# A decoder layer in fp32 on one core: another order of the second feed-forward matrix's products, a fixed PSUM place for each of their sums, attention output operands made by halves, and the first unit's weight sums shared otherwise between two engines

## The chip, the cores and the metric

One core of a Trainium2 chip runs the whole kernel. The metric is the device time in microseconds of one execution, taken as the median of several runs. The engines that matter are TensorE (PE, with its weight loads PEld), VectorE (DVE), ScalarE (ACT), GpSimd (POOL) and SyncE (SP), which here does nothing but issue DMAs. All data are fp32; a matrix product of fp32 operands shows in the trace as two PE instructions.

## The reference: what is computed

The input `x` has shape (4, 2048, 512): four time steps T, 2048 rows B, 512 features D. One decoder layer is applied:

```python
x = x + ssm(layernorm(x))              # a linear recurrence over the 4 time steps
x = x + cross_attention(layernorm(x), ctx_1024, Wq, Wk, Wv, Wo)   # 16 heads of 32, 77 keys
x = x + ffn(layernorm(x))

def ffn(x):
    h = x @ W_exp + b_exp              # 512 -> 2048
    h = butterfly(h, up_weights)       # 11 stages of 2x2 blocks
    h = gelu(h + up_bias)
    h = butterfly(h, down_weights)
    return h @ W_con + b_con + down_bias   # 2048 -> 512
```

The butterflies are linear, so the kernel first multiplies them into the two matrices. What remains of the feed-forward part is one matrix 512 x 2048, a gelu, and one matrix 2048 x 512.

## The kernel before, in words

**Stages.** A preparation of some 197 us builds the two feed-forward matrices (`_prepare`), keys and values, and the operands of the other projections. Then 16 units follow, each of 128 rows at all four time steps. For unit u, `feed_forward(u, xt, rhs, other)` runs the two feed-forward matrices, and `other` is the generator `front(u + 1, ...)`: recurrence, attention and norm of the next unit. Inside `feed_forward`, `step()` is called after every 4 PE instructions or so, and it advances `other` at a fixed rate, 56 advances over 98 steps (90 in unit 0, which starts with 8 steps without any). So PE alternates between the two units, and each unit takes about 154 us. The last unit, 15, has no `other`.

**Who orders the work.** The program is written in one order, and a scheduler places each engine's instructions from it by their dependencies and by its own idea of durations; each engine then runs its queue strictly in that order. Only in the preparation (PE, SP and POOL) and in the first four columns of unit 0 (PE) is the written order kept, and where `tc.keep_in_program_order` says so.

**First matrix** (`up_head`, `up_mid`, `up_tail`, lines 777 to 826). Eight columns p, seven block products each (Strassen's scheme), with weights of 896 KB from `up7` that SP loads in `up_weights` (L1013). Three accumulators with PSUM tags a, b, c are reused within a column, so PE waits for DVE's reads (L799, L811, L812, L820, L823). ACT applies the gelu (L785).

**Second matrix** (the loop over `plan` in `feed_forward`). 26 products, each 4 fp32 matmuls (8 PE instructions, L876) of 128 x 256. `DOWN` gives their order: the product's number, the name of the sum in PSUM that it is added to, and where that sum then goes ("+20" is row block t = 2, left half of the features, added; two or three targets make one wide DVE instruction). A sum keeps its name over several products, and what comes later under the same name is added on top of what was there: DVE adds the running value to `xt` (L891) or subtracts it (L893), and the next product of that name has to wait until DVE has read. The sum's PSUM place was taken in rotation over the tags a, b, c (two buffers each) when a name first appeared.

The left operands are sums of the activations (`SUMS`, `LEFT`), made on POOL (`made`, L833), 1.3 us each, 28 per unit. `_down_plan` places them: each sum is emitted so that it stands four products ahead of the product that needs it, and it is written to the place that came free first, be it one of nine spare places or the block of an activation that is no longer needed.

The right operands are 26 blocks of the second matrix in DRAM (`dn26`), loaded two by two on SP (L869). They are made only once: `_right_sums` forms 18 sums of blocks for one of four row sets, `_right_stores` writes them to DRAM (L152). Set 0 is done in the preparation, all on POOL (L140); sets 1 to 3 in unit 0 after columns 0 to 2, where the names in `FAST` go to DVE (L142). Both use the same two rings in SBUF, so a set has to wait for the stores of the one before. SP issues these stores ahead of the weights of column 4, since columns 0 to 3 were loaded ahead.

**Attention output** (end of the loop over t in `front`, then `sw`). For each time step ACT computes exponentials (L680), DVE the sums (L678, L682, L683), PE transposes the probabilities (L695) and multiplies by the values into `ps_o` (L705). DVE copies that to `ot` (L707). After the fourth copy, four sums of quarters of `ot` are made, two on DVE (L714, L715) and two on POOL (L716, L717), and the seven products with `wo` follow (L615), whose results DVE adds to `xt` (L724, L728).

**Norm.** `norm_stats` (L536 to L549) is a chain on DVE: four statistics of 128 x 512, then thirteen tiny instructions of 128 x 4 with three Newton steps. `normed` then scales rows (L562), PE transposes them (L571), ACT copies them out (L572). `normed_pairs` does the same for the recurrence (L589, L600, L601). After its own front, each unit from 1 on computes the statistics of the next `x` in advance (`stats`); unit 1's are computed at the start of its front, in unit 0.

**Bias and stores.** The output bias `ybias` is added to `xt` on POOL: quarter rows in each column (L848), in unit 0 two additions of 128 x 1024 in columns 5 and 7 (L851). The result rows are stored from SP (L859): rows 0, 1, 2 after product 17, halves of row 3 after product 6 and at the end. Units' `xt` live in three buffers, so the load of unit u + 2 (L528) waits for the stores of unit u - 1.

Of the kernel before, what the change touches and what calls it, by code (L numbers as in the profile page):

```python
# [14 lines left out]
ALU = mybir.AluOpType  # L15
AX = mybir.AxisListType

P = 128
T, B, D = 4, 2048, 512
# [48 lines left out]
DOWN = ((11, "x", "+01"), (12, "y", "+30"), (5, "x", "+00"), (16, "y", "+31"), (1, "p", "+11"), (18, "q", "+20"),  # L68
# [4 lines left out]

# [7 lines left out]
PLAIN = tuple(f"b{k}{n}" for k in range(4) for n in range(2))  # L81
FAST = "24", "5", "1", "8"
SLOT = {name: i for i, name in enumerate([row[0] for lot in RIGHT for row in lot] + list(PLAIN))}
# [418 lines left out]
def kernel(ctx: ExitStack, tc: tile.TileContext, x, ctx_t, ssm_vec, ssm_vt, ssm_vinv, wq_t, wk_t, wv_t,  # L502
                        wo_t, wexp_t, up_low, up_high, up_bias, dn_low, dn_high, wcon, b_con, down_bias, out):
    nc = tc.nc
# [13 lines left out]
    ybias = const.tile([P, D], F32, name="ybias")  # L518
# [101 lines left out]
    def front(u, xt, res, wq=None):  # L620
# [47 lines left out]
        ot = work.tile([P, NC, T, P], F32, tag="xnt", bufs=2, name="ot")  # L668
        for t in range(T + 1):
# [32 lines left out]
            for g in range(NC):  # L702
                for j in range(4):
                    h = 4 * g + j
                    nc.tensor.matmul(po[j * DH : (j + 1) * DH, g, :], lhsT=vsb[:, tt, h * DH : (h + 1) * DH],  # L705
                                     rhs=pts[0:NK, g, j, :], start=True, stop=True, tile_position=(0, j * DH))
            nc.vector.tensor_copy(ot[:, :, tt, :], po)  # L707
            yield
# [4 lines left out]
        s1, s2, s3, s4 = (sw[:, i] for i in range(4))  # L713
        nc.vector.tensor_tensor(s1, a21, a22, ALU.add)  # L714
        nc.vector.tensor_tensor(s2, s1, a11, ALU.subtract)  # L715
        nc.gpsimd.tensor_tensor(s3, a11, a21, ALU.subtract)  # L716
        nc.gpsimd.tensor_tensor(s4, a12, s2, ALU.subtract)  # L717
        yield
# [32 lines left out]
    def feed_forward(u, xt, rhs, other):  # L751
# [17 lines left out]
        def bank(tag):  # L769
            return psum.tile([P, 512], F32, tag=tag, name=f"ps_{tag}")  # L770
# [64 lines left out]
        for p in range(h):  # L835
# [5 lines left out]
            if u == 0 and p < 3:  # L841
                _right_sums(nc, p + 1, wdn, rings, False)
                _right_stores(nc, p + 1, wdn, rings, dn26, (0, 1, 2))
# [3 lines left out]
            if u:  # L847
                tc.keep_in_program_order(nc.gpsimd.tensor_tensor(r, r, ybias[:, d], ALU.add))  # L848
            elif p % 2 and p > h // 2:
                r = xt[:, p - 5 : p - 3, :]  # L850
                tc.keep_in_program_order(nc.gpsimd.tensor_tensor(r, r, ybias.unsqueeze(1).to_broadcast([P, 2, D]), ALU.add))  # L851
            if p >= h // 2:
                made(*plan.pop(0)[1:])
        up_tail(h - 1)

        sums, banked, pair = {}, 0, None

        def store(t, d=slice(0, D)):
            nc.sync.dma_start(out=out[t, u * P : (u + 1) * P, d], in_=xt[:, t, d])  # L859

        for kind, where, *rest in plan:
# [9 lines left out]
            if first:  # L871
                sums[name] = bank("abc"[banked % 3])[:, 0 : D // 2]
                banked += 1
            ps, left = sums[name], place(where)
# [6 lines left out]
            while goes:  # L881
# [10 lines left out]
                else:  # L892
                    nc.vector.tensor_tensor(r, r, x, ALU.subtract)  # L893
            for t, when in enumerate((17, 17, 17)):
                if i == when:
                    store(t)
            if i == 6:
                store(3, slice(0, D // 2))
        store(3, slice(D // 2, D))
        for _ in other:  # L900
# [28 lines left out]
    with ExitStack() as stack, tc.manual_schedule(engines={E.PE, E.SP, E.Pool}):  # L929
# [45 lines left out]
        for n, _ in enumerate(prep):  # L975
            if n == 27:
                _right_sums(nc, 0, wdn, rings, True)
            if n == 31:
                _right_stores(nc, 0, wdn, rings, dn26, (2, 0))
# [114 lines left out]
```

## Time and profile before

| | us |
|---|---|
| median of 3 runs | 2631.2 (2629.01 to 2632.6) |
| the profiled execution | 2631.95 |
| its span, first to last instruction | 2630.2 |
| mean granted clock of PE | 0.993 |

| stage | from, to (us) |
|---|---|
| preparation, with the front of unit 0 | 0 to 197 |
| unit 0, with the front of unit 1 | 197 to 382 |
| units 1 to 14, some 154 us each | 382 to 2534 |
| unit 15 alone | 2534 to the end |

A line of the profile that groups instructions gives source line, engine, operation, and the program's names of output and inputs (buffer numbers left out). In a view by order of time the first two numbers are the start and the duration in us, and in brackets stands how long the engine was idle before and what ended the idle time. In a view of waits the three numbers are the total in us, how many times, and the longest. In a view by windows each engine's busy time in the window is followed by its number of instructions, and the last three numbers are the granted clock of PE, the mean share in which the DMA engines were busy, and GB/s. Of an engine's idle time only PE's is a loss by itself.

### The profile page before, as it was taken

The numbers are of one execution on the slowest core, as the hardware profiler recorded it, in microseconds if no ns is written. First come the engines' busy times: TensorE is split into PE (matmuls) and PEld (weight loads), VectorE is DVE, ScalarE is ACT, GpSimd is POOL, SyncE is SP. The second block draws the span as 40 slices with busy tenths as digits, with TensorE's granted clock in tenths as the row PEclk, the third lists the DMA queues.
The fourth block names the chain that finished last, engine by engine and source line by source line (L and its number), as shares of the span: only waits on it lengthen the run. The fifth ranks groups of instructions, "written<-read, shape, count | busy, mean of one in ns | idle before, by whom it ended". The sixth has DMA issues, their size and how long they took to land.

```text
span 2630.2 us, 39485 instructions
## 1 busy us (share of the span) xinstructions
PE 2526.9 (96%) x14280; PEld 2126.0 (81%) x14280; DVE 1599.6 (61%) x3480; ACT 1039.9 (40%) x3263; POOL 935.2 (36%) x851
## 2 busy tenths in 40 slices
PE   8896999999999999999999999999999999999999
PEld 5775878787888878788887878888787887878788
DVE  6657475755747575574747557474755747565553
ACT  2442524336262433626244362624436262443621
POOL 4437231514233151423415242341524234152434
PEclk9997999999999999999999999999999999999999
DMA  5718443454535345453544545453454544444456
GB/s 178 254 68 309 143 159 142 156 177 153 200 140 173 144 154 179 153 200 141 166 149 151 184 152 198 143 168 145 151 186 153 196 145 159 149 153 171 154 171 238
DMA packets 143220, 440.71 MB, mean 168 GB/s; under 512 B 20657, under 2 KB 48433, under 8 KB 140209
## 3 DMA queue, kind: packets, MB, share of 16 engines
q1 hardware_dynamic: 143026, 438.18, 48.2%
q8 instruction: 115, 1.88, 0.3%
q14 instruction: 79, 0.65, 0.1%
HBM read 398.27 MB, written 39.86 MB: 167 GB/s over the span
## 4 chain that ended last, share of the span: by engine, by line
PE 76%; DVE 14%; ACT 7%; issue 1%; DMA 1%; POOL 1%; SPq 0%; DVEq 0%; ACTq 0%; POOLq 0%
PE ps_b L780 11%; PE ps_a L876 9%; PE ps_a L780 7%; PE ps_q L615 7%; PE ps_c L780 7%; PE ps_c L876 6%; PE ps_w L615 5%; PE ps_b L876 4%; PE ps_pt L695 3%; PE ps_sc L675 3%; ACT pr L680 3%; PE ps_s L630 3%; PE ps_o L705 3%; PE ps_t L571 2%; DVE st L536 2%; ACT L785 1%
## 5 line engine op out<-in xcount | busy, mean ns | idle before, releaser
L833 POOL TENSOR_TENSOR arena<-arena 128x512 f32<-128x512 f32 x448 | 601.2, 1348 | 1288.8 <-ACT arena L785 780.8
L785 ACT ACTIVATE arena<-arena,hbias 128x256 f32<-128x256 f32 x384 | 191.7, 507 | 338.8 <-DVE arena L820 263.6
L680 ACT ACTIVATE pr<-ps_sc,low 128x77 f32<-128x77 f32 x960 | 297.1, 331 | 48.3 <-DVE low L678 46.0
L780 PE MATMUL ps_b<-arena 128*128 128x256 f32 x1128 | 293.2, 380 | 8.7 <-issue 5.4
L572 ACT COPY xnt<-ps_t 128x512 f32<-128x512 f32 x128 | 72.1, 585 | 474.2 <-PE ps_t L571 474.2
L780 PEld LDWEIGHTS ps_b<-arena 128*128 128x128 f32 x1128 | 207.6, 190 | 40.8 <-issue 10.6
L876 PE MATMUL ps_a<-arena 128*128 128x256 f32 x896 | 223.2, 379 | 0.0
L680 ACT ACTIVATION_READ_ACCUMULATOR pr<-ps_sc,low 128x1 f32 x960 | 203.2, 212 | 0.0
L780 PE MATMUL ps_a<-xnt,arena 128*128 128x256 f32 x752 | 196.4, 380 | 1.3 <-ACT arena L785 1.3
L876 PEld LDWEIGHTS ps_a<-arena 128*128 128x128 f32 x896 | 165.7, 190 | 26.4
L876 PE MATMUL ps_c<-arena 128*128 128x256 f32 x768 | 184.4, 380 | 0.2
L678 DVE TENSOR_REDUCE low<-ps_sc 128x4 f32<-128x308 f32 x240 | 114.8, 478 | 101.5 <-PE ps_sc L675 96.0
L675 PE MATMUL ps_sc<-kbd,qt 128*128 128x308 f32 x480 | 166.6, 434 | 0.0
L876 PE MATMUL ps_a<-w,arena 128*128 128x256 f32 x512 | 133.8, 385 | 30.1 <-DVE xt L893 15.7
L876 PEld LDWEIGHTS ps_c<-arena 128*128 128x128 f32 x768 | 144.0, 190 | 22.8 <-DMA arena<-dn 2.5
L780 PEld LDWEIGHTS ps_a<-xnt,arena 128*128 128x128 f32 x752 | 143.3, 191 | 23.6 <-ACT arena L785 1.6
L796 ACT COPY arena<-ps_a 128x256 f32<-128x256 f32 x128 | 48.2, 376 | 274.6 <-PE ps_a L780 274.6
L615 PE MATMUL ps_q<-xnt,wq 128*128 128x256 f32 x640 | 151.2, 379 | 2.2 <-POOL xnt L660 2.2
L695 PE MATMUL ps_pt<-ident,pr 128*77 128x128 f32 x1024 | 148.6, 278 | 4.0 <-DVE pt L700 4.0
L695 PEld LDWEIGHTS ps_pt<-ident,pr 128*77 128x77 f32 x1024 | 116.9, 147 | 37.6 <-DVE pt L700 10.0
L820 DVE TENSOR_TENSOR arena<-ps_b,arena 128x256 f32<-128x256 f32 x128 | 54.0, 422 | 137.1 <-PE ps_b L780 137.1
L615 PEld LDWEIGHTS ps_q<-xnt,wq 128*128 128x128 f32 x640 | 121.4, 190 | 19.1 <-POOL xnt L660 2.6
(232 smaller groups left out, 5007.2 us busy)
## 6 DMA issues: line engine op xcount, KB each, us to landing
arena<-dn SPq DMA_DIRECT2D x256, 512.0 KB, 4.3
w<-dn SPq DMA_DIRECT2D x160, 512.0 KB, 3.7
arena<-up SPq DMA_DIRECT2D x79, 896.0 KB, 4.5
wq<-wq SPq DMA_DIRECT2D x16, 1792.0 KB, 8.4
w<-up SPq DMA_DIRECT2D x32, 896.0 KB, 6.3
xt<-in_x SPq DMA_DIRECT2D x11, 1024.0 KB, 7.2
dn<-arena SPq DMA_DIRECT2D x8, 1152.0 KB, 5.1
out<-xt SPq DMA_DIRECT2D x33, 256.0 KB, 5.9
```

The costliest lines, as they stand in the source:

```text
L572: nc.scalar.copy(xnt[:, :, t, :], ps)
L615: nc.tensor.matmul(tiles[key][:, r, :], lhsT=lhs(i, r, k), rhs=rhs(i, r, k), start=key == i and r == 0 and k == 0, stop=k == 1, skip_group ...
L630: nc.tensor.matmul(ps[:, 2 * i : T, f * NS : (f + 1) * NS], lhsT=xpt[:, i, c * (P // NS) + f, :], rhs=gt[:, 0 : T - 2 * i, :], start=i == ...
L675: nc.tensor.matmul(ps[:, 0 : 4 * NK], lhsT=qt[:, g, t, :], rhs=kbd[:, t, g, :], start=True, stop=True)
L678: nc.vector.tensor_reduce(low, sc, AX.X, ALU.min)
L680: nc.scalar.activation(pr[:, 4 * g + h, :], sc[:, h, :], AF.Exp, bias=low[:, h : h + 1], scale=-1.0, accum_out=sm[:, 4 * g + h : 4 * g + h ...
L695: nc.tensor.transpose(pt_ps[0:NK, j, :], pr[:, 4 * g + j, :], ident)
L705: nc.tensor.matmul(po[j * DH : (j + 1) * DH, g, :], lhsT=vsb[:, tt, h * DH : (h + 1) * DH], rhs=pts[0:NK, g, j, :], start=True, stop=True, ...
L780: nc.tensor.matmul(ps, lhsT=w[:, c, :], rhs=rhs[i - 1][:, c], start=first and c == 0, stop=c == 1, skip_group_check=True)
L785: nc.scalar.activation(out, x, AF.Gelu, bias=hbias[:, b : b + 1])
L833: nc.gpsimd.tensor_tensor(place(p), place(x), place(y), ALU.add if op == "+" else ALU.subtract)
L876: nc.tensor.matmul(ps, lhsT=left[:, j, :], rhs=pair[:, n, j, :], start=first and j == 0, stop=j == NB // 4 - 1, skip_group_check=True)
```

## The change

1. `DOWN` has another order from the 11th product on, the sum "p2" is called "o", and each sum's PSUM tag is fixed by `BANK` in place of the rotation. The planner's sums follow the new order.
2. In unit 0 the right sums of set 1 go to POOL alone, and `FAST` sends eight names instead of four to DVE in sets 2 and 3.
3. The copy of `ps_o` to `ot` goes from DVE to ACT, and the four sums `s1` to `s4` are made in two halves, for t = 0 and 2 and for t = 1 and 3.
4. In unit 0 the bias additions are eight of 128 x 256, in columns 6 and 7.
5. The statistics of `x` of unit 1 are computed in the preparation.
6. The stores: rows 1 and 2 after product 19, the left halves of rows 0 and 3 after product 6, the right half of row 0 after product 23, that of row 3 at the end.

```diff
-        (22, "r", "+31"), (13, "p2", "+00"), (25, "w", "+00"), (14, "x", "+10 +11"), (3, "v", "+20"),
-        (15, "y", "+21 +20"), (7, "w", "+20"), (24, "v", "+00 +10"), (20, "z", "+31"), (8, "u", "-00 -10"),
-        (9, "w", "+21"), (10, "z", "+11"), (4, "u", "+21"), (21, "s", "+01 +11 +21"), (19, "z", "+10"), (23, "w", "+01"),
-        (17, "t", "+10 +30 -01 -21"), (2, "z", ""), (6, "z", "+30"), (0, "u", "+31"))
+        (22, "r", "+31"), (13, "o", "+00"), (25, "w", "+00"), (14, "x", "+10 +11"), (15, "y", "+21 +20"), (3, "v", "+20"),
+        (20, "z", "+31"), (7, "w", "+20"), (8, "u", "-00 -10"), (10, "z", "+11"), (24, "v", "+00 +10"),
+        (21, "s", "+01 +11 +21"), (17, "t", "+10 +30 -01 -21"), (9, "w", "+21"), (4, "u", "+21"), (19, "z", "+10"),
+        (2, "z", ""), (6, "z", "+30"), (23, "w", "+01"), (0, "u", "+31"))
+BANK = dict(x="a", y="b", p="c", q="c", r="c", o="c", w="a", v="b", z="a", u="b", s="c", t="c")
...
-FAST = "24", "5", "1", "8"
+FAST = "24", "5", "1", "8", "14", "2", "20", "10"
...
-            nc.vector.tensor_copy(ot[:, :, tt, :], po)
+            nc.scalar.copy(ot[:, :, tt, :], po)
...
-        nc.vector.tensor_tensor(s1, a21, a22, ALU.add)
-        nc.vector.tensor_tensor(s2, s1, a11, ALU.subtract)
-        nc.gpsimd.tensor_tensor(s3, a11, a21, ALU.subtract)
-        nc.gpsimd.tensor_tensor(s4, a12, s2, ALU.subtract)
+        for q in (slice(0, 1), slice(1, 2)):
+            nc.vector.tensor_tensor(s1[:, :, q], a21[:, :, q], a22[:, :, q], ALU.add)
+            nc.vector.tensor_tensor(s2[:, :, q], s1[:, :, q], a11[:, :, q], ALU.subtract)
+            nc.gpsimd.tensor_tensor(s3[:, :, q], a11[:, :, q], a21[:, :, q], ALU.subtract)
+            nc.gpsimd.tensor_tensor(s4[:, :, q], a12[:, :, q], s2[:, :, q], ALU.subtract)
...
-                _right_sums(nc, p + 1, wdn, rings, False)
+                _right_sums(nc, p + 1, wdn, rings, p == 0)
...
-            elif p % 2 and p > h // 2:
-                r = xt[:, p - 5 : p - 3, :]
-                tc.keep_in_program_order(nc.gpsimd.tensor_tensor(r, r, ybias.unsqueeze(1).to_broadcast([P, 2, D]), ALU.add))
+            elif p >= h - 2:
+                for t in (2 * p - 12, 2 * p - 11):
+                    for d in (slice(0, D // 2), slice(D // 2, D)):
+                        added = nc.gpsimd.tensor_tensor(xt[:, t, d], xt[:, t, d], ybias[:, d], ALU.add)
+                        tc.keep_in_program_order(added)
...
-                sums[name] = bank("abc"[banked % 3])[:, 0 : D // 2]
-                banked += 1
+                sums[name] = bank(BANK[name])[:, 0 : D // 2]
...
-            for t, when in enumerate((17, 17, 17)):
-                if i == when:
-                    store(t)
+            if i == 19:
+                store(1)
+                store(2)
             if i == 6:
+                store(0, slice(0, D // 2))
                 store(3, slice(0, D // 2))
+            if i == 23:
+                store(0, slice(D // 2, D))
         store(3, slice(D // 2, D))
...
+            if n == 36:
+                stats[1] = norm_stats(xts[1], tc.keep_in_program_order)
```

More of the change, by code (lines that the diff above doesn't have):

```diff
@@ L854, in feed_forward @@
         up_tail(h - 1)
-        sums, banked, pair = {}, 0, None
+        sums, pair = {}, None
         def store(t, d=slice(0, D)):
```

## The prediction

> **What bounds the kernel now.** I read the page's engine shares first, then the waits of the matmul engine by stretch, then one steady unit in order of time on each engine, then the start of the first unit.
>
> ```profile
> PE 2526.9 (96%) x14280; PEld 2126.0 (81%) x14280; DVE 1599.6 (61%) x3480; ACT 1039.9 (40%) x3263; POOL 935.2 (36%) x851
> ```
>
> PE is the bound. No edit changes its instruction count, so all that can be won is its idle time, some 103 us of 2630.2, and the places where its clock is low. Waits of PE from 500 us on, where units 1 to 14 pass the place in question, and unit 15 without another unit beside it:
>
> ```profile
> PE ps_a L876 <- DVE xt L893: 15.7, 9, 1.8
> PE ps_a L876 <- DVE arena L893: 8.7, 5, 1.8
> PE ps_w L615 <- DVE sw L715: 6.8, 13, 0.5
> PE ps_a L876 <- ACT arena L785: 5.4, 13, 0.4
> PE ps_b L780 <- issue: 5.0, 13, 0.4
> PE ps_t L571 <- DVE xn L562: 2.9, 14, 0.2
> PE ps_o L705 <- DVE pt L700: 2.6, 14, 0.2
> ```
>
> Columns: total us, times, longest. Fourteen times PE waits 1.75 us for one VectorE subtraction at L893. Around it, in the unit near 1200 us, PE, then DVE, then POOL:
>
> ```profile
> 1288.10 1.13 PE L876 MATMUL ps_a<-w,arena 128*128 128x256 f32 x4 [1.75 <-DVE xt L893]
> 1289.44 0.63 PE L571 MATMUL ps_t<-ident,xn 128*128 128x128 f32 x4 [0.21 <-DVE xn L562]
> ```
> ```profile
> 1283.64 1.11 DVE L547 TENSOR_TENSOR w<-y,v 128x4 f32<-128x4 f32 x1
> 1284.79 0.16 DVE L548 TENSOR_TENSOR w<-w,y 128x4 f32<-128x4 f32 x1
> 1284.98 1.12 DVE L549 SCALAR_TENSOR_TENSOR y<-w,y 128x4 f32<-128x4 f32 x1
> 1286.14 0.16 DVE L547 TENSOR_TENSOR w<-y,v 128x4 f32<-128x4 f32 x1
> 1286.34 1.11 DVE L548 TENSOR_TENSOR w<-w,y 128x4 f32<-128x4 f32 x1
> 1287.37 0.68 DVE L893 TENSOR_TENSOR xt<-xt,ps_a 128x512 f32<-128x512 f32 x1
> ```
> ```profile
> 1279.53 7.90 POOL L833 TENSOR_TENSOR arena<-arena 128x512 f32<-128x512 f32 x6 [10.78 <-PE ps_b L876]
> ```
>
> PE must add product 4 to the sum "u" that product 8 left; the subtraction that reads it stands on DVE behind the Newton steps of the norm. Of those, every second one takes 1.1 us instead of 0.16, as long as POOL runs its six operand sums. The same chain ends in the row L562 that the transposes need. So two waits lie on each other: take only the first away and PE stands at L571. Last, the start of the first unit, as windows (PE, PEld, DVE, ACT, POOL, clock, DMA share):
>
> ```profile
> 215.00:220.00 5.00, 0.23 (x2) 0.00 (x0) 3.83 (x12) 0.00 (x0) 3.03 (x4) 0.58 0.92 310
> 220.00:225.00 5.00, 1.00 (x5) 1.03 (x6) 4.89 (x9) 0.00 (x0) 4.92 (x7) 0.50 1.04 342
> 250.00:255.00 5.00, 0.06 (x1) 0.09 (x2) 4.86 (x6) 0.00 (x0) 4.12 (x3) 0.50 1.05 443
> ```
>
> Here PE idles for 8.77 us (for xp L589) and 7.15 us (for xn L562), both behind the norm on DVE beside a busy POOL.
>
> **What the Trainium skill says.** "SBUF — State Buffer", Who interferes with whom: a DVE instruction with two SBUF inputs, or in a two-port mode, and a GpSimd instruction that reads SBUF take one port in turn, for a whole instruction. The trace agrees: 0.16 against 1.11 us above, while evictions with one PSUM input keep 0.42. "TensorE: Matmul & The Clock Gate", What's actually happening: an idle window of some 3.4 us halves the clock, and about as much work restores it. Agrees: 0.50 after both stalls, four matmuls in 1.91 instead of 1.03. "VectorE: DVE Perf Modes", The TRN2 errata: copying 512 fp32 from PSUM is (120+512)/0.96 = 658 ns on DVE and (172+512)/1.2 = 570 ns on ScalarE; the trace has 0.69 (L707) and 0.58 (L572).
>
> **The change part by part.**
>
> Product order and fixed places. Each product is 8 PE instructions, 1.73 us; PE reaches L571 in the middle of the 19th product in either order. Before, 8 and 4 stood 16th and 19th with two products between them; now 15th and 21st with five, 8.6 us instead of 3.5. The wait for L893 was 3.5 + 1.75 after product 8 ended, so it goes: 24.4 us. What is late next is the row at L571, ready at 1289.30, where PE without the stall would be at 1287.05: 2.25 us would remain, more than the stall. It depends on POOL. By the planner's rule the new order asks for the sums of the late products (7, 8, 9, 24, 21, 17) from operands and places that come free by the 12th product, so some 16 sums of 1.3 us run from about 1250 to 1266, and POOL then waits for the 18th product (1286.2). Without POOL the thirteen steps L542 to L549 take 0.2 us each, 2.6, as they do at 1303 to 1306, against 6.5 here (7.15 less 0.6 for L893). Five evictions now fall into the chain (0.42, 0.68, 0.42, 0.66, perhaps 0.96) where there were three (0.66, 0.39, 0.68): +0.5 to +1.4. Row at 1289.30 - 3.9 + 1.0 = 1286.4, before PE at 1287.05. So the 2.9 us go too. If half of the sums stay in the window, the row comes at 1287.3 to 1288.4, 0.3 to 1.3 us per unit left.
>
> New wait: 2 follows 19 directly on "z", so its first matmul waits until DVE has evicted 19: 0.42 + about 0.1 if DVE is free, 1.8 more if it stands behind L745 (1.79). Queued behind it on PE: the rest of the unit. PE's order is the scheduler's, which already hoists (the 2nd product runs before the 1st), and 23 or the next unit's first product can go between: 0 to 2.3 us, I take 0.4, 14 x 0.4 = 5.6 back. The other places: "r" needs "p" evicted one product earlier; bounded by one DVE multiply L683 (up to 2.37), hidden by the hoisting; 0.
>
> Operands by step, copy of ot to ScalarE. L615 waits 0.52 for L715 (1.64 us beside POOL L716). Now the halves for t = 0 and 2 are made before the last copy; after it remain 0.58 (ACT), and two halves of 0.41 (as L142), from 1264.3 to 1265.7, or 1267.1 if each meets a POOL half of 0.72 (as L848). PE would want the first half at 1267.03 and this one four matmuls (0.86) later: the wait goes, 7.8 us in all (15). Halves cost 0.13 more each on DVE, 0.17 on POOL, beside PE. The copy takes 0.69 x 64 = 44 us from DVE, puts 37 on ACT; ACT stands idle after each ps_o (0.99, 2.87, 3.07 us and 26 after the last), so 0. Without that cover it would be up to 0.58 x 4 x 15 = 35 us.
>
> Stores: six instead of five on SP per unit; behind them weights that land far ahead: 0, at the end too, since the last store is the same half row (0.3 either way).
>
> First unit. Statistics of x1 move ahead of the first product, into DVE's idle 4.03 us before 197.46 and the 3.28 that L142 leaves there; they cost 5.3 us alone, up to 10 beside POOL; in the second case L799 of the first product is 2 us late. Set 1 of the right sums goes wholly to POOL: 4 more of 0.74; it frees L368, for which PE waits 2.50. Sets 2 and 3 give four more each to DVE (0.41): POOL has 38 instead of 42, 3.0 us less, DVE 16 instead of 12. The bias additions (two of 2.34) become eight of 0.72 and come one step later: +1.1 us of POOL, but shorter blocks of the port. Waits that could go: 2.50 + 8.77 + 7.15, with some 6 us of half clock. But p = 4 needs weights that SP issues behind the nine right-sum stores, at 241.04, landing 4.5 later, 245.6, at most 3.0 earlier; DMA is near full share from 205 to 250. p = 4 starts now at 258.52, so the gain is at most 12.9 to 15.9, less some 2 of half clock after the idle that is left: I take 11, bounds 0 (DVE blocked by L142 waiting for a store) and 16. In the first unit's second matrix the row wait of 2.89 (POOL: four sums, 5.18) goes by 2.6.
>
> **Sum.** 24.4 + 2.9 + 7.8 - 5.6 + 2.6 + 11 = 43.1. From the profiled execution's 2631.95 that gives 2588.9; it lies 0.75 over the median of 2631.2, so 2588.
>
> **The rivals.** One: the row takes the place. POOL's sums stay beside the norm chain, L571 inherits the stall, and only L615 (7.8), 0.3 a unit (4) and half of the first unit (7) are won, 18.8: 2612. For it: both waits end on one DVE chain. Against: the planner's rule. Two: all goes, z is filled, and the small waits of 0.39 on L780 behind L589 go too (5): 29.5 + 5.6 + 5 + 2.6 + 16 = 58.7: 2572. Three, slower: the eviction of 19 stands on DVE behind the next unit's statistics, 7 us long (1298.94 to 1306), and PE waits for it at 2. It decides from 43.1/14 + 0.4 = 3.5 us a unit; at 5 us it is 14 x 4.6 - 43 = 21 slower: 2652. For it: just such a place cost "u" 4.5 us after its product. Against: 19 ends at about 1294, before those statistics. Four: DVE's relief was hidden and the first unit's weights decide; within 5 us.
>
> **Chances.** Forecast 0.56, one 0.21, two 0.13, three 0.06, four 0.04. A measurement here tells 0.2%, 5 us, from none: faster 0.90, same 0.04, slower 0.06. The range of 2567 to 2615 takes in one and two and leaves out three and four.
>
> **What would show it.** Right: no PE wait on L893; L571 waits under 0.3 a unit; L615 none on sw; POOL's sums in one block before L716, none beside L542 to L549; L600's wait of 8.77 and the half clock after it gone, with a wait for weights or rows near 240 to 245. Wrong: L571 with 1 to 2 us a unit, a wait of PE on L891 at the last products, or p = 4 at 255 or later.

## The result, and the profile after

| | before | after |
|---|---|---|
| median | 2632.21 us (20 runs) | 2639.48 us (20 runs, 2635.63 to 2646.15) |
| ratio to before | | 1.0024, interval 1.0013 to 1.0034 |
| the profiled execution, its span | 2631.95, 2630.2 us | 2642.55, 2640.8 us |

Slower by 0.24%, where 1.6% faster was forecast. 2639.5 is outside the range, and of the rivals only the third lies on that side. The shares of the engines, first:

```profile
PE 2537.6 (96%) x14280; PEld 2127.7 (81%) x14280; DVE 1519.4 (58%) x3452; ACT 1071.6 (41%) x3327; POOL 924.2 (35%) x885
```

DVE has lost 80 us and PE has gained 11: that DVE has less to do did not by itself make the kernel shorter. Next the waits of PE from 500 us on, in the same columns (total, times, longest); most lines are one higher than before, those of the feed-forward two or three.

```profile
PE ps_o L706 <- DVE pt L701: 18.1, 26, 1.0
PE ps_a L879 <- DVE xt L894: 11.4, 9, 1.3
PE ps_a L879 <- DVE arena L894: 6.2, 5, 1.3
PE ps_w L616 <- DVE sw L717: 5.0, 13, 0.4
PE ps_c L879 <- DMA arena<-dn: 2.9, 3, 1.7
```

The 24.4 us on the subtraction (L893 before, L896 now) and the 2.9 on L571 are gone, as forecast. In their place stand 17.6 us (11.4 and 6.2) at product 2, which follows product 19 on the sum z, and 18.1 at `ps_o`, which was 2.6. The same unit as before, near 1200 us, on DVE:

```profile
1282.53 0.16 DVE L548 TENSOR_TENSOR w<-y,v 128x4 f32<-128x4 f32 x1
1282.72 0.16 DVE L549 TENSOR_TENSOR w<-w,y 128x4 f32<-128x4 f32 x1
1282.80 0.42 DVE L894 TENSOR_TENSOR xt<-ps_a,xt 128x256 f32<-128x256 f32 x1
1283.14 0.15 DVE L550 SCALAR_TENSOR_TENSOR y<-w,y 128x4 f32<-128x4 f32 x1
...
1293.65 1.79 DVE L747 TENSOR_TENSOR arena<-xnt 128x512 f32<-128x512 f32 x1 [0.70 <-ACT xnt L573]
1295.55 0.69 DVE L749 TENSOR_TENSOR arena<-xnt,arena 128x512 f32<-128x512 f32 x1
1296.15 0.69 DVE L537 BATCH_NORM_STATS2 st<-arena 128x6 f32<-128x512 f32 x1
1296.76 0.41 DVE L894 TENSOR_TENSOR xt<-ps_a,xt 128x256 f32<-128x256 f32 x1
```

Above the dots, the Newton steps: 0.16 us each where every second one took 1.1. That part is right. Below, the last line is the eviction of product 19. It stands behind the combination sums of the next unit's operands (L747, L749) and one of the next unit's statistics, and PE waits for it, after six of the eight instructions of product 23 (the first line):

```profile
1294.50 1.46 PE L879 MATMUL ps_a<-w,arena 128*128 128x256 f32 x6
1297.22 3.07 PE L879 MATMUL ps_a<-arena 128*128 128x256 f32 x13 [1.26 <-DVE xt L894]
```

The sums of POOL, which no longer lie beside the norm, lie here:

```profile
1249.83 9.49 POOL L835 TENSOR_TENSOR arena<-arena 128x512 f32<-128x512 f32 x6 [1.50 <-PE ps_a L879]
1259.29 0.90 POOL L718 TENSOR_TENSOR sw<-ot 128x256 f32<-128x256 f32 x1
1260.16 4.02 POOL L835 TENSOR_TENSOR arena<-arena 128x512 f32<-128x512 f32 x3
1264.14 0.90 POOL L719 TENSOR_TENSOR sw<-ot,sw 128x256 f32<-128x256 f32 x1
```

That is the attention output of the next unit. What lay there in the kernel before, on POOL and then on DVE (the multiply of the softmax, the second operand sum):

```profile
1250.25 9.08 POOL L833 TENSOR_TENSOR arena<-arena 128x512 f32<-128x512 f32 x6 [1.46 <-PE ps_a L876]
1256.26 1.95 DVE L683 TENSOR_TENSOR pr<-pr,sm 128x1232 f32<-128x1232 f32 x1
1265.76 1.64 DVE L715 TENSOR_TENSOR sw<-sw,ot 128x512 f32<-128x512 f32 x1
```

And in after, on DVE, the same multiply and the second halves of the two sums:

```profile
1253.39 1.71 DVE L684 TENSOR_TENSOR pr<-pr,sm 128x1232 f32<-128x1232 f32 x1
1262.03 1.02 DVE L716 TENSOR_TENSOR sw<-ot 128x256 f32<-128x256 f32 x1 [1.49 <-ACT ot L708]
1263.08 1.37 DVE L717 TENSOR_TENSOR sw<-sw,ot 128x256 f32<-128x256 f32 x1
```

So six of POOL's sums lay there before as well; the move made the stretch longer and denser. The two second halves end 2.4 us after the last copy of `ot`, as late as the two whole sums did before. Last, the stretches of the first unit's start in after's windows (columns as before), with the one from 250:

```profile
215.00:220.00 5.00, 4.09 (x24) 3.31 (x23) 4.90 (x8) 0.59 (x1) 4.45 (x6) 1.00 0.93 317
220.00:225.00 5.00, 4.37 (x25) 3.78 (x26) 4.96 (x9) 2.60 (x6) 3.62 (x5) 1.00 0.75 251
250.00:255.00 5.00, 5.00 (x17) 4.06 (x17) 2.56 (x3) 0.94 (x2) 4.35 (x5) 0.69 0.97 388
```

PE works where it stood idle, and the recurrence of unit 1 starts at 221.15 instead of 232.80 us.

**Where the time came from.** A way of counting used below: from PE's records, the time from one instruction's start to the next beyond what is usual for that line and width, summed over a unit and put down to the later one's line. It includes half clock and the filling of the pipeline, so it is more than the waits. A unit's period is the distance from one recurrence to the next; "steady" is its median over units 1 to 13.

| | before | after |
|---|---|---|
| start of unit 0's first product | 197.01 | 193.60 |
| start of unit 1's recurrence | 232.80 | 221.15 |
| period of unit 0 | 160.74 | 162.69 |
| steady period | 153.60 | 154.72 |
| lost at `ps_o`, L706 | 3.11 | 4.39 |
| lost at `ps_w`, L616 | 1.05 | 1.43 |
| lost at scores and transposes, L676 and L696 | 1.49 | 2.43 |
| lost at second matrix, L879 | 2.70 | 2.45 |
| lost at first matrix and norm, L782 and L572 | 1.26 | 0.22 |

So a start 11.7 us earlier is more than spent by 1.1 us in each of the later units, by 2 in unit 0, by 2 in what follows the last recurrence, and by another 1.5 to 2.2 in each of three units where weights landed late.

### The profile page after: what moved, and what is told of

It reads as the page before. It is cut to its first block, busy times and chain, and to the rows that moved or that the text cites. A ratio compares the mean times of both kernels' runs of the same rounds, so it can differ in the third digit from the quotient of the medians.

```text
span 2640.8 us, 39542 instructions
## 1 busy us (share of the span) xinstructions
PE 2537.6 (96%) x14280; PEld 2127.7 (81%) x14280; DVE 1519.4 (58%) x3452; ACT 1071.6 (41%) x3327; POOL 924.2 (35%) x885
## 4 chain that ended last, share of the span: by engine, by line
PE 77%; DVE 10%; ACT 8%; DMA 2%; POOL 1%; issue 1%; DVEq 0%; POOLq 0%; ACTq 0%; SPq 0%
PE ps_a L879 11%; PE ps_b L782 11%; PE ps_a L782 7%; PE ps_q L616 7%; PE ps_c L782 7%; PE ps_b L879 6%; PE ps_c L879 6%; PE ps_w L616 6%; ACT pr L681 4%; PE ps_sc L676 3%; PE ps_s L631 3%; PE ps_pt L696 3%; PE ps_o L706 2%; PE ps_t L572 2%; ACT L787 1%; ACT L681 1%
## 5 line engine op out<-in xcount | busy, mean ns | idle before, releaser
L835 POOL TENSOR_TENSOR arena<-arena 128x512 f32<-128x512 f32 x448 | 593.6, 1336 | 1457.8 <-ACT arena L787 822.3
L782 PE MATMUL ps_b<-arena 128*128 128x256 f32 x1128 | 293.8, 381 | 3.8 <-DVE arena L813 3.8
L879 PE MATMUL ps_a<-arena 128*128 128x256 f32 x896 | 220.0, 381 | 18.8 <-DVE xt L894 12.7
L782 PEld LDWEIGHTS ps_b<-arena 128*128 128x128 f32 x1128 | 209.8, 191 | 31.3 <-DVE arena L813 4.2
L879 PEld LDWEIGHTS ps_a<-arena 128*128 128x128 f32 x896 | 165.5, 190 | 50.0 <-DVE xt L894 16.7
L879 PE MATMUL ps_b<-arena 128*128 128x256 f32 x768 | 201.4, 380 | 0.5 <-DVE xt L894 0.5
L782 PE MATMUL ps_a<-xnt,arena 128*128 128x256 f32 x752 | 196.3, 380 | 0.0
L676 PE MATMUL ps_sc<-kbd,qt 128*128 128x308 f32 x480 | 170.2, 442 | 0.0
L879 PE MATMUL ps_a<-w,arena 128*128 128x256 f32 x640 | 160.9, 382 | 5.9 <-ACT arena L787 5.8
L782 PEld LDWEIGHTS ps_a<-xnt,arena 128*128 128x128 f32 x752 | 143.3, 191 | 22.0
L696 PE MATMUL ps_pt<-ident,pr 128*77 128x128 f32 x1024 | 153.4, 279 | 4.2 <-DVE pt L701 3.9
L616 PE MATMUL ps_q<-xnt,wq 128*128 128x256 f32 x640 | 151.2, 379 | 2.2 <-POOL xnt L661 2.2
L696 PEld LDWEIGHTS ps_pt<-ident,pr 128*77 128x77 f32 x1024 | 119.2, 147 | 41.8 <-DVE pt L701 15.7
L879 PEld LDWEIGHTS ps_b<-arena 128*128 128x128 f32 x768 | 137.6, 190 | 16.0 <-DVE xt L894 0.9
L879 PEld LDWEIGHTS ps_a<-w,arena 128*128 128x128 f32 x640 | 118.8, 190 | 26.8 <-ACT arena L787 11.4
L616 PEld LDWEIGHTS ps_q<-xnt,wq 128*128 128x128 f32 x640 | 121.5, 190 | 19.0 <-POOL xnt L661 2.6
```

The source lines that it names most:

```text
L616: nc.tensor.matmul(tiles[key][:, r, :], lhsT=lhs(i, r, k), rhs=rhs(i, r, k), start=key == i and r == 0 and k == 0, stop=k == 1, skip_group ...
L676: nc.tensor.matmul(ps[:, 0 : 4 * NK], lhsT=qt[:, g, t, :], rhs=kbd[:, t, g, :], start=True, stop=True)
L696: nc.tensor.transpose(pt_ps[0:NK, j, :], pr[:, 4 * g + j, :], ident)
L782: nc.tensor.matmul(ps, lhsT=w[:, c, :], rhs=rhs[i - 1][:, c], start=first and c == 0, stop=c == 1, skip_group_check=True)
L835: nc.gpsimd.tensor_tensor(place(p), place(x), place(y), ALU.add if op == "+" else ALU.subtract)
L879: nc.tensor.matmul(ps, lhsT=left[:, j, :], rhs=pair[:, n, j, :], start=first and j == 0, stop=j == NB // 4 - 1, skip_group_check=True)
```

## The experiments

The theory after the traces, P, is that each unit has three new costs, each with its own cause: (1) the fixed place for "r" takes away a filler ahead of the first `ps_o`; (2) product 2 follows product 19 on its place; (3) POOL's moved sums meet DVE's work of the attention output, halves included. The rival, A, is that the copy of `ot` on ScalarE makes the loss. A third reading is that the first unit's edits win nothing that lasts. The first four kernels undo one part of the change or do one part alone.

**e1: rotation in place of the fixed places.**

```diff
-                sums[name] = bank(BANK[name])[:, 0 : D // 2]
+                sums[name] = bank("abc"[banked % 3])[:, 0 : D // 2]
+                banked += 1
```

> The changed kernel with the rotation over the tags a, b, c put back in place of the fixed places; all else as changed. Theory P (places): with "r" bound to tag c, product 22 can no longer stand ahead of the first attention output product, so PE has nothing to run while DVE copies the transposed probabilities; with the rotation three quarters of product 22 stand there again (1.3 us), the wait of 1.0 us a unit at that place goes, and the time falls by 15 x 1.0 to 1.3, to 2620 to 2625. Rival A (ScalarE copy): the wait comes from the copy of ot that went to ScalarE, and stays: 2637 to 2642.

2626.55 us, ratio to before 0.9975 (0.9966 to 0.9984). Steady 153.89, 0.83 less than after. What filled PE ahead of the first `ps_o` in the kernel before, and what is left of it in after:

```profile
1233.28 0.60 PE L876 MATMUL ps_b<-arena 128*128 128x256 f32 x2
1233.71 1.46 PE L876 MATMUL ps_b<-w,arena 128*128 128x256 f32 x6
1235.10 1.08 PE L705 MATMUL ps_o<-pt,vsb 77*32 77x128 f32 x32
```
```profile
1228.84 0.60 PE L879 MATMUL ps_b<-arena 128*128 128x256 f32 x2
1230.45 1.08 PE L706 MATMUL ps_o<-pt,vsb 77*32 77x128 f32 x32 [1.01 <-DVE pt L701]
```

The six instructions of 1.4 us are three quarters of product 22, "r". With "r" on tag c, behind "p" and "q" on the same tag, its place isn't free yet. With rotation they stand there again and the first `ps_o` has no wait. But the third and the last one now wait, 0.32 and 0.81:

```profile
PE ps_o L706 <- DVE pt L701: 15.9, 28, 0.8
```

So cause (1) is shown, at 0.83 us a unit net. The edit frees the places of all the sums; that it is "r" that counts is read from these lines. Little of the gain is at `ps_o` itself (4.39 to 4.28 lost), since the later ones take up most of what the first one gives; `ps_w` falls from 1.43 to 0.89. The waits at `ps_o` have a second cause.

**e2: the copy of `ot` back on VectorE.** `nc.scalar.copy(ot[...], po)` is `nc.vector.tensor_copy` again.

> The changed kernel with the copy of ps_o to ot back on VectorE; all else as changed. Rival A: the waits at the attention output, at the transposes of the probabilities and at the scores go back to what they were, 2.2 us a unit less: 2606 to 2612. Theory P: the wait of 1.0 us at the first attention output product of a unit stays; only the small losses at the scores and transposes (0.5 and 0.4 us a unit) can go: 2626 to 2636, and the waits of the operand sums for the attention output grow by 0.1 each.

2638.59 us, 1.0027 (1.0017 to 1.0037): as after. Scores and transposes fell back from 2.43 to 1.52 us a unit, and `ps_w` rose from 1.43 to 2.11. `ps_o` rose by 0.21. The copy on ScalarE isn't free: it costs 0.9 where the exponentials and the copies of pt stand on the same queue, and wins about as much at `ps_w` and `ps_o`. Rival A falls. The steady period is 154.57, so the copy explains 0.15 of the 1.1.

**e3: the first unit's edits alone**, in the kernel before: `FAST`, set 1, bias additions, statistics in the preparation.

> The kernel before with the first unit's edits alone: right sums shared otherwise, statistics of unit 1 in the preparation, bias additions in quarter rows; order, places, copy and stores as before. If these edits gave the 11.6 us that the first unit's recurrence comes earlier in the changed kernel, and no unit pays for it later: 2618 to 2623. If the gain is given back in the same unit's second matrix (the next 160.8 us became 162.7): 2621 to 2625. If it came from the order of the products: 2629 to 2634.

2626.85 us, 0.9981 (0.9970 to 0.9992): 6 us are won, though unit 1's recurrence starts at 220.30, 12.5 earlier than in before's trace. Unit 0 is 3.2 longer, the steady period is 153.71.

**e4: order, places and stores alone**, in the kernel before.

> The kernel before with the new product order, the fixed places and the stores that go with it; first unit, copy and operand sums as before. Theory P: the norm's wait at L571 and the wait of 1.75 us for the subtraction go (2.2 us less a unit), 1.0 comes at the first attention output product and some 1.3 at the product that follows product 19 on sum z: within 5 us of 2632. Rival A: no new wait at the attention output: 2610 to 2620. If the step sums and not the order made POOL's sums fall into the attention output, they wait here as before (0.5).

2637.2 us, 1.0019 (1.0011 to 1.0027). Without halves, copies and first unit, the order with its places is by itself slower. Its waits, from 375 us on:

```profile
PE ps_w L616 <- DVE sw L716: 20.8, 14, 1.5
PE ps_o L706 <- DVE pt L701: 14.2, 14, 1.0
PE ps_a L876 <- DVE xt L891: 11.4, 9, 1.3
PE ps_a L876 <- DVE arena L891: 6.2, 5, 1.3
```

All three new costs are here; the third shows as the old wait for the whole sums at `ps_w`, which has grown from 0.52 to 1.49: the first sum (L715 here, L714 before) took 1.67 us beside POOL's sums instead of 0.69. The steady period is 154.29, so in the fixed places the copies and the halves together cost only the 0.43 that remain to after's 154.72. Yet unit 1's recurrence starts at 225.98 in this kernel, which has none of the first unit's edits. More on that at e8.

**e5: 19 four products ahead of 2**, on top of e1 (rows 1 and 2 are stored after 4):

```diff
-        (21, ...), (17, ...), (9, ...), (4, ...), (19, "z", "+10"), (2, "z", ""), (6, "z", "+30"),
+        (21, ...), (19, "z", "+10"), (17, ...), (9, ...), (4, ...), (2, "z", ""), (6, "z", "+30"),
```

> The kernel after with its places dealt out in rotation, and product 19 moved from directly ahead of 2 to a place four products earlier (21, 19, 17, 9, 4, 2); rows 1 and 2 are stored after product 4. Theory P (2 follows 19 on its place, 1.26 us a unit behind the next unit's combination sums on VectorE): the wait at the z products goes, 14 x 1.26 = 17.6, nothing takes its place; a steady period of 152.6 us instead of 153.87, and 2609 us, 17 less than the rotation alone (2626.6). Rival R (VectorE's backlog at that point is what holds PE, so another eviction of the last products or the first of the next unit's expansion inherits the wait): the period stays above 153.4 and the time above 2620.

2609.41 us, 0.9912 (0.9899 to 0.9926), 17 less than e1, as expected. Steady 152.91; the second matrix loses 0.69 instead of 2.52. What remains at that place is 0.3 a unit at the next unit's first product:

```profile
PE ps_a L782 <- DVE xt L895: 2.8, 9, 0.3
PE ps_a L782 <- DVE arena L895: 1.2, 4, 0.3
```

Cause (2) is shown, about 1.0 us a unit net.

**e6: whole sums** on top of e1, s1 to s4 as in the kernel before.

> The kernel after with its places in rotation and the four operand sums of the attention projection made whole, as in the kernel before. Theory Q (the first halves stand on VectorE ahead of the last copy of pt, so the last ps_o waits 0.81 us a unit for them): that wait goes, and ps_w waits for the whole sums instead, 1.0 to 1.5 us a unit; the time within 5 us of the rotation alone (2626.6). Rival S (the last ps_o waits because the softmax multiply on VectorE is drawn out to 2.5 us by GpSimd's sums, whatever the halves do): the wait stays at 0.7 or more and ps_w adds 0.5 to 1.0 to it; 2634 to 2642.

2624.46 us, 0.9965 (0.9952 to 0.9977). `ps_o` loses 3.48 instead of 4.28, `ps_w` 1.36 instead of 0.89: what the halves win at `ps_w` they cost ahead of the last `ps_o`.

**e7: GpSimd kept quiet** on top of e1. From unit 1 on, the kernel leaves out some 18 of the 28 operand sums of a unit, so what it writes is not the layer's result; PE's work is the same.

```diff
             if kind == "sum":
-                made(where, *rest)
+                if not u or done < 3 or done > 17:
+                    made(where, *rest)
```

> The kernel after with its places in rotation, which in units 1 to 15 leaves out the operand sums on GpSimd that the plan puts from the third to the seventeenth product of the second matrix, some 18 of 1.3 us a unit (their operands are what an earlier unit left there). Theory T (these sums, moved out of the norm's chain, now draw out VectorE's work in the attention output): the multiply L684 falls from 2.5 to about 1.6 us, the first half L717 from 1.4 to 0.5, the ps_o waits from 0.8 a unit to under 0.3 and ps_w to under 0.5 a unit; a steady period of 152.5 or less instead of 153.87, and 2608 us or less. Rival U (the order of the queue alone makes these waits): the period within 0.4 of 153.87 and the time within 6 us of 2626.6.

2603.32 us, 0.9890 (0.9876 to 0.9903). Steady 152.31, 1.58 less than e1. In e1, then in e7, the multiply of the softmax and the first half of s2:

```profile
1252.54 2.50 DVE L684 TENSOR_TENSOR pr<-pr,sm 128x1232 f32<-128x1232 f32 x1
...
1258.08 1.38 DVE L717 TENSOR_TENSOR sw<-sw,ot 128x256 f32<-128x256 f32 x1
```
```profile
1236.97 1.44 DVE L684 TENSOR_TENSOR pr<-pr,sm 128x1232 f32<-128x1232 f32 x1
...
1241.97 0.83 DVE L717 TENSOR_TENSOR sw<-sw,ot 128x256 f32<-128x256 f32 x1
```

The waits at `ps_o` are 0.3 a unit, that at `ps_w` is gone, that at product 2 stays at 1.2. Cause (3) is shown, but 1.58 is a bound for what the move costs: the kernel takes away all sums of this stretch, of which six were there before the change, with 1.95 us for the same multiply. And the price depends on where the two engines meet: with the fixed places of after the multiply took 1.71, and the halves more. L717 fell to 0.83 and not to the 0.5 expected; POOL's own halves are still beside it.

**e8: the first unit's sums alone**, in the kernel before: `FAST` and set 1 only.

> The kernel before with the other sharing of the first unit's right-hand sums alone (four more sums each of sets 2 and 3 on VectorE, set 1 wholly on GpSimd); statistics and bias additions stay as before. Theory V (the sums decide when the last weights are stored and when p = 4 starts): at least 8 of the 12.5 us that the three edits together took from the first unit's start are here; stores end 4 to 6 us earlier; 2626 to 2629. Rival W (the earlier statistics are the larger part): the first unit's front starts within 4 us of before's 232.8, and the time is above 2629.

2633.94 us, 1.0004 (0.9996 to 1.0011), so no difference, and neither V nor W: the recurrence starts at 226.46. But e4 starts it at 225.98 and the later e11 at 226.56, with no edit of the first unit. It is before's 232.80 that stands out. Windows of 130 to 160 us, of before and of e11:

```profile
130.00:160.00 30.00, 26.36 (x243) 22.05 (x242) 17.74 (x27) 16.28 (x76) 7.92 (x5) 0.89 0.13 43
```
```profile
130.00:160.00 30.00, 26.36 (x265) 22.84 (x264) 18.75 (x28) 16.91 (x76) 9.10 (x6) 1.00 0.13 43
```

In before's execution the clock was halved for 6.8 us there, in the preparation, where e11 has the same code: both show PE busy for 26.36 us, and before gets through 22 instructions less in it. Against after's trace this stretch is the whole of the 3.4 us: the two run level up to 132 us. Over the fifteen kernels of this study unit 0's first product starts at anything from 190.6 to 200.5 us. So the first unit has to be measured from there. From its first product to unit 1's recurrence it is 35.8 us in before, 33.2 in e4, 34.2 in e11 and 33.2 in e8; with all the edits it is 27.3 (e3), 27.6 (after, e12), and 26.5 to 27.6 in all eleven kernels that have them. The other sharing of the sums by itself wins nothing; the edits together win some 6 to 9 us, of which unit 0's period gives 2 to 3 back (before to after, before to e3, e11 to e12). The second of the two weight transfers that SP issues behind the stores goes out 45.7 us after the first product in before, 43.7 and 44.1 in e4 and e11, 43.0 in e8, and 42.5 to 43.3 in e3, after and e12. That is 0.4 to 1.5 earlier if it is taken from e4 and e11, and 2.3 to 3.1 if it is taken from before, so how far the queue was released is not shown.

**e9: only the last copy on ScalarE**, on top of e5; **e10: the same with whole sums.**

```diff
-            nc.scalar.copy(ot[:, :, tt, :], po)
+            (nc.scalar.copy if tt == T - 1 else nc.vector.tensor_copy)(ot[:, :, tt, :], po)
```

> The kernel of the z gap (places in rotation, 19 four products ahead of 2), with only the last of the four copies of ot on ScalarE and the other three back on VectorE. Theory X (the copies on ScalarE stand ahead of the exponentials and of the copies of pt, which costs PE 0.5 us a unit at the scores and 0.35 at the transposes; only the last copy needs ScalarE, since it stands right ahead of the operand sums): a steady period of 152.1 us instead of 152.9, L676 at about 0.85 a unit, L696 at 0.65, ps_w as it is (0.8); 2597 us. Rival Y (VectorE's 0.69 each comes back at ps_o and ps_w, as it did with all four copies on VectorE): the period within 0.3 of 152.9; 2605 to 2613.

> The same with the four operand sums of the attention projection made whole again. Theory X with Q (halves cost the last ps_o what they win at ps_w): 0.2 us a unit less than with halves, as between the two with rotation, so some 3 us less than the last one, 2594. Rival Y2 (with more copies on VectorE the whole sums come later and ps_w waits 1.5 us a unit, as in the run of the order and places alone): 0.5 us a unit or more over the last one, 2604 or more.

e9 is 2616.17 us, 0.9946 (0.9930 to 0.9961), 7 more than e5, and theory X with its 2597 is wrong. Scores and transposes fell as X says (2.35 to 1.50), but `ps_w` rose from 0.78 to 1.96. The sums on DVE, first and second halves, with PE's waits:

```profile
1250.92 0.90 DVE L716 TENSOR_TENSOR sw<-ot 128x256 f32<-128x256 f32 x1
1251.86 1.37 DVE L717 TENSOR_TENSOR sw<-sw,ot 128x256 f32<-128x256 f32 x1
1253.15 0.68 DVE L701 COPY pt<-ps_pt 77x512 f32<-77x512 f32 x1
1255.70 1.50 DVE L716 TENSOR_TENSOR sw<-ot 128x256 f32<-128x256 f32 x1 [1.88 <-ACT ot L708]
```
```profile
1253.88 1.08 PE L706 MATMUL ps_o<-pt,vsb 77*32 77x128 f32 x32 [0.98 <-DVE pt L701]
1258.66 1.13 PE L616 MATMUL ps_w<-wo,sw 128*128 128x256 f32 x4 [0.91 <-DVE sw L717]
```

The two first halves, 2.3 us, stand ahead of the last copy of pt, for which PE waits 0.98. The two second halves take 1.50 and 1.37 us beside POOL, where e5 had 0.91 and 0.83, and PE waits for them too. e10 takes them away: 2598.69 us, 0.9877 (0.9860 to 0.9894), steady 151.96 instead of 153.13, no wait at any `ps_o`. So here the halves cost 1.17 us a unit, far more than the 0.2 expected from e6. `ps_w` waits 1.33 for the whole sums, nearly the 1.5 of Y2, and it still is the faster kernel, by 1.2 us a unit, which neither reading had.

**e11: the order alone**, in the kernel before: the new order with 19 four products ahead of 2, rotation, the stores.

> The kernel before with the new order of products alone, 19 four products ahead of 2, places in rotation; copies, operand sums and first unit as before. Theory P with T (the order takes 2.0 us a unit off the second matrix and 0.4 off L571, and gives back 1.1 at ps_w, where GpSimd's sums now draw out the operand sums, and 0.3 at ps_o): a steady period of 152.6 us instead of 153.6, and 2612 to 2618 us. Rival T2 (the sums' new place costs all that the order wins): the period at 153.3 or more and the time above 2625.

2597.94 us, 0.9875 (0.9859 to 0.9891), 14 us below the lower end of what was expected. Steady 151.63. Its only wait of size at the attention output:

```profile
PE ps_w L616 <- DVE sw L716: 12.6, 14, 0.9
```

Against e10 the last copy is back on DVE and the first unit's edits are out; e12 below differs from e10 in the copy alone and has 151.67, so the copy is worth 0.29 a unit. The sums are ready at the same distance from the last `ps_o` in both (ps_w begins on them 4.77 and 4.76 us after it starts), but in e11 PE has 0.86 us of the second matrix to do in between, in e10 0.43. Why the scheduler puts less there was not tried.

**e12: e11 with the first unit's edits.**

> The kernel of the order alone (2597.9) with the three edits of the first unit (sharing of the sums, statistics of the second unit in the preparation, bias additions by quarters). Theory Z (the parts add: the first unit's start comes 6 us earlier than with the order alone, as between the first-unit kernel's 220.3 us and the 226.6 of both the order alone and the sums alone, and the next period gives back some 3): 2593 to 2596. Rival Z2 (what the start wins is lost again to weights that land late in the steady units, as the first-unit edits alone kept 5 of 12.5): 2597 to 2602.

2592.79 us, 0.9855 (0.9835 to 0.9875), the fastest kernel here, 5.2 below e11, as e3 is 5.8 below the 2632.6 of before that was run beside it. Each is the median of four executions, and the two intervals just overlap, but the times do not (at most 2595.3 in e12, at least 2596.9 in e11). So the parts add, as theory Z has it, and Z2 falls: some 5 us of what the first unit wins last.

**e13: after with whole sums alone.**

> The kernel after with only the four operand sums made whole again (fixed places, all copies on ScalarE, 19 right ahead of 2). Theory Q (halves cost at the last ps_o what they win at ps_w when all four copies are on ScalarE): the last ps_o's 0.38 us a unit goes, ps_w waits 0.8 to 1.2 us for the whole sums instead of 0.4; 2634 to 2640. Rival S2 (the halves cost 1.16 us a unit, as they do with three copies on VectorE): a steady period of 153.5 instead of 154.68; 2620 to 2626.

2634.77 us, 1.0016 (1.0008 to 1.0024); steady 154.28. The last `ps_o`'s wait is gone, `ps_w` waits 0.84. In the changed kernel itself the halves cost 0.44 us a unit. So Q is near where all copies are on ScalarE (0.44 here, 0.22 from e1 to e6), and S2's price is met only in e10, with three on VectorE.

## Why the prediction was wrong

Two of its large terms were right, and they are what e11 has. L893's wait and L571's, 27.3 us or 1.95 a unit in the forecast, were won: with the order, rotation and the gap at 19, and nothing else, the period falls by 1.97. That the two numbers meet so closely is in part luck, since e11 also waits 0.38 more at `ps_w` and wins a little elsewhere. POOL's sums left the norm as predicted, ten of them to 1250 to 1266, where some 16 were forecast; the Newton steps take 0.16, L572 doesn't wait. What failed is what was put at nothing (the fixed places, the sums' new neighbours, the copies on ACT) or too low (product 2 behind 19), and what the halves hold up on DVE.

The forecast's steady terms (24.4 + 2.9 + 7.8 - 5.6) are 2.1 us a unit of gain; measured is a loss of 1.1, so 3.2 are to be explained. A chain of kernels, each one edit from the next, accounts for nearly as much. It ends at another kernel than the one forecast (without halves and without copies on ACT), and the price of an edit depends on what is already in place:

| from, to | steady period | a unit |
|---|---|---|
| after to e1: rotation | 154.72 to 153.89 | 0.83 |
| e1 to e5: 19 ahead of 2 by four products | 153.89 to 152.91 | 0.98 |
| e5 to e9: three copies back on DVE | 152.91 to 153.13 | -0.22 |
| e9 to e10: whole sums | 153.13 to 151.96 | 1.17 |
| e10 to e12: the last copy back on DVE | 151.96 to 151.67 | 0.29 |
| sum | | 3.05 |

The steps that failed, as the prediction put them:

- **"'r' needs 'p' evicted one product earlier; ... hidden by the hoisting; 0."** This is the wrong way round. The hoisting is what hides other waits, and it needs a free place. Product 22 did not itself come late; it was no longer there to fill the gap in which DVE copies pt. Forecast 0, measured 0.83 a unit.
- **"I take 0.4, 14 x 0.4 = 5.6 back."** The mechanism was named, and so was its bound of 0 to 2.3; the size was off. The eviction of 19 stands behind L747, L749 and one statistic, and PE waits 1.26 us a unit for it, 17.6 in all. This is rival three's place, at a third of the price from which rival three was to decide. PE did hoist 23 in front, but six instructions of it are 1.3 us and were not enough. The argument against, that 19 ends before the statistics, left out the combination sum that the prediction had itself named at this place (L745, 1.79); it stands earlier in the queue, and a second sum and one of the statistics came ahead of the eviction too.
- **Where the sums of POOL go.** The prediction counted what the norm gains from their leaving, and nothing for the neighbours they get. At 1250 to 1266 lies the attention output with L684, L716 and L717 on DVE, all with two SBUF inputs. e7 puts the price at no more than 1.58 a unit, over e1. "SBUF — State Buffer", Who interferes with whom, in the Trainium skill, has the rule that the prediction itself used for the norm: one port pair, held for a whole instruction. The traces agree in the new place too, with 2.50 us in e1 against 1.44 in e7 for the same multiply.
- **"The wait goes, 7.8 us in all."** It shrank to 0.38, and 0.4 (e13) to 1.2 us (e9, e10) a unit were paid for that elsewhere, net. The second halves were to end 0.8 us after the last copy of `ot`, or 2.2 if each met a POOL half; they met POOL's operand sums and ended 2.4 after it, and PE waited. What was left out besides is what is queued behind the first halves on DVE: the last copy of pt.
- **"ACT stands idle after each ps_o ..., so 0."** The cover was read from ACT's idle time. In the changed kernel the copy costs 0.9 a unit at scores and transposes (e2), 14 us over 15 units, two fifths of the bound of 35 that was given. About as much came back at `ps_w` and `ps_o`, which the term did not have either; net it is 0.15.
- **First unit, 11.** By the medians it is 5 to 6 (e12, e3). The stalls of 8.77 and 7.15 shrank to 0.91 and 3.99 as thought, but new waits of 5.29 at L801 behind the statistics and 3.85 at L813 took their place: the statistics took 12.5 us beside POOL (190.97 to 203.5) where "up to 10" was allowed, so L801 was 5 late and not 2. Column p = 4 started at 249.74 instead of 258.52, 8.8 earlier and not 11, and 3.4 of that stood ahead of unit 0: the start from which the 11 was taken was one execution's, with half clock in its preparation. Whether the weights of p = 4 went out the 3.0 earlier that the 11 leans on stays open (e8).

That the kernel is slower at all turns on the places: undo them alone and it is 0.25% faster than before (e1); undo the halves alone (e13) or the copies alone (e2) and it stays slower. The pair of edits at the attention output costs 0.43 a unit in the changed kernel (e4), where the halves alone cost 0.44 and the copies alone 0.15; with rotation and the gap at 19 it costs 1.24 (e5 to e12). So what looked small there was the largest loss left once the others were gone. Left open: why weights land late in three units of after (1.66 us at the longest), which no kernel here tried.

## What to carry to other kernels

An edit that takes work away from one stretch of a queue puts it into another: price the stretch where it lands by the same rule by which you priced the one it left. A product that can be hoisted is a filler, and its accumulator's place is what lets it be hoisted; before places are fixed, list which waits are short only because such a product stands in front. And for a stage that runs once, take its times from several executions or sister kernels before forecasting a gain from it.

## What was not expected of the hardware

Half clock came after shorter idle times than "TensorE: Matmul & The Clock Gate", What's actually happening, suggests with its idle window of some 3.4 us. In e3, in a unit like all others:

```profile
510.10 1.13 PE L878 MATMUL ps_a<-w,arena 128*128 128x256 f32 x4 [1.74 <-DVE xt L895]
511.44 1.04 PE L571 MATMUL ps_t<-ident,xn 128*128 128x128 f32 x4 [0.21 <-DVE xn L562]
512.28 1.92 PE L878 MATMUL ps_a<-w,arena 128*128 128x256 f32 x4
```
```profile
506.00:511.00 5.00, 3.26 (x15) 2.40 (x14) 4.72 (x11) 0.00 (x0) 3.27 (x3) 1.00 0.83 268
511.50:514.90 3.40, 3.40 (x11) 2.86 (x12) 2.17 (x5) 0.58 (x1) 3.40 (x5) 0.50 0.14 57
```

After waits of 1.74 and 0.21 us PE had half its clock for 3.4 us, and four matmuls took 1.92 instead of 1.03. The length is that of the page, and so is a window that runs on by itself: in e3's trace half clock begins at 235.0, 511.5, 975.7 and 2054.3 us, which lie 81, 136 and 316 times 3.413 us apart. But of the 3.4 us ahead of 511.5 PE had been idle for about 2, not for all.

The rhythm also tells which waits had this price, some 2 us each. In the steady units of before, e3 and e8 the same two waits stand 42 times. Cut into stretches of 3.413 us on each trace's own rhythm, both fell into one stretch five times (PE idle for 1.90 to 1.95 us of it, three times in e3 and twice in e8), and half clock followed each time; in the other 37 places no stretch had more than 1.75 us of idle time, and it never did. Idle time alone is not the whole rule: in e13 a wait of 1.0 at `ps_o` followed by a late weight did it twice, with 1.2 us idle in the stretch. In before, too, the half clock that the prediction took for agreement began at 215.8 us, only 0.6 us into the stall of 8.77.
